# A two-layer graph network on 64 images: the first batch's convolution transform as TensorE products, its outputs finished by quarters

## The chip, the cores and the metric

The kernel runs on one core of a Trainium2 chip. The metric is device time in microseconds (us) of one execution, lower is better. Before the change it is 2314.8 us (median of three runs, 2313.39 to 2315.6). Runs are compared with runs of the kernel before on the same chip.

Engine names in the profile: PE is TensorE (matrix products and transposes), PEld its weight load, DVE VectorE, ACT ScalarE, POOL GpSimd, SP the engine that issues most loads.

## The reference, cut to what matters

There are 64 images of 256 nodes with 256 features. Each goes through two convolutions along the nodes, a distance-weighted message passing, a gated update, and a second layer of one aggregation with a layer norm.

```python
xc = jnp.transpose(x, (0, 2, 1))
h = jax.nn.relu(_bn(_conv1d(xc, conv1_w, 0), ...))       # 1 tap
h = _bn(_conv1d(h, conv2_w, 8), ...)                      # 17 taps: "conv2"
x_conv = jnp.transpose(jax.nn.relu(h + xc), (0, 2, 1))
s = x @ w_se.T + b_se                                     # 3 coordinates per node
A = jnp.exp(-dist) * mask                                 # dist from s
x_nmp = A @ jax.nn.relu(x @ w_msg.T + b_msg)
# gates r, z, n from [x_conv, x_nmp] and x; then the second layer (cut)
```

## The kernel before

conv2 is not computed tap by tap. Tiles of 32 nodes are taken to a transform domain (slots V, U, S and S2 of a large tile XF), multiplied there slot by slot with transformed filters on PE (`ps_k`), and taken back (the "inverse"). The transform, the merges of the products and the inverse are additions on DVE. Eight images form a batch and share this work: DVE's instructions cover all eight.

One product group uses three PSUM banks. The results leave them by `take`, one copy on ACT and two instructions on DVE:

```python
    def products(b, first, sums):
        p1, p2, p3 = bank("ps_k1"), bank("ps_k2"), bank("ps_k3")
        ...
        def take():
            nc.scalar.copy(k1, p1)
            nc.vector.tensor_sub(sl(re, 2)..., k1, p3)
            nc.vector.tensor_add(sl(im, 2)..., k1, p2)
```

All PSUM tiles of the kernel come from one pool of eight banks.

The convolution of the *next* batch is a generator that yields estimated costs. It is dealt out at ten points ("pumps") per image between the work of the images of *this* batch:

```python
    def cost(n):
        return 0.15 + 0.265 * n
    ...
        share, spent = (39.0 if b == 0 else 61.0) / len(todo), 0.0   # between two product groups of a batch
    ...
    for b in range(NB):
        coming = conv(b + 1) if b + 1 < NB else iter(())
        done, at, goal = 0.0, 0, BG * POINTS - 6
        def pump():
            nonlocal done, at
            at += 1
            while done < total * at / goal:
                t = next(coming, 1e9)
                if t is None:
                    break
                done += t
        for k in range(b * BG, (b + 1) * BG):
            ...                     # the image's own work, with ten pump() between
        for _ in coming:            # whatever is left is emitted here, in one block
            pass
```

`total` is not a constant. It is what batch 0's own convolution cost while it was emitted at the start:

```python
    first, total = conv(0), 0.0
    ...
        total += next(first)
        for i in range(n_groups):
            next(fl)                # one step of making the filters
            while total < FRONT * (i + 1) / n_groups and 0 not in STAGE:
                total += next(first) or 0.0
```

The "front" below means everything until the first gates: filters, batch 0's convolution, the first messages. A "seam" is the passage from the last image of one batch to the first of the next. There are seven.

## Time and profile before

| stretch of the kernel before | length, us | PE busy | DVE busy |
|---|---|---|---|
| start to first products (110.35) | 110.35 | 84.2 | 64.8 |
| products of batch 0 and merges (to 165) | 54.65 | 46.4 | 49.7 |
| inverse of batch 0 (to the first gates, 190.2) | 25.2 | 15.3 | 20.9 |
| one steady batch length (456 to 723) | 267 | 263.2 | 206.0 |

The last row is how the table is to be read: over 267 us PE did 263 us of work, so only work taken off PE or gaps of PE can shorten it. In the first three rows PE idles 44 us together; this is what the change is after.

### The profile page before, as it was taken

How to read it: one execution, taken by the hardware profiler on the slowest of the kernel's cores; microseconds unless marked ns; L12 is line 12 of the kernel's file. 1: busy time of each engine (PE TensorE's matmuls, PEld its weight loads, DVE VectorE, ACT ScalarE, POOL GpSimd, SP SyncE). 2: the span in 40 equal slices, each digit the busy share in tenths (PEclk: the TensorE clock that was granted, in tenths of full speed). 3: DMA queues.
4: the chain of work that ended last, by engine and by line, in shares of the span. 5: the costliest groups of instructions: out<-in, count | busy, mean ns of one | idle time of the engine just before them, and what ended most of it. 6: DMA issues, size and time to landing. Idle time of an engine off the chain costs nothing.

```text
span 2314.6 us, 24215 instructions
## 1 busy us (share of the span) xinstructions
PE 2225.2 (96%) x8262; PEld 1456.2 (63%) x8262; DVE 1685.2 (73%) x3212; ACT 766.0 (33%) x1577; POOL 468.7 (20%) x925
## 2 busy tenths in 40 slices
PE   7879999999999999999999999999999999999996
PEld 4565566666666666666666566665666656666663
DVE  2893998759794788829887498956889398874543
ACT  4514222442224321353224332253223532243332
POOL 1000221312122222202212131221222122121211
PEclk8998999999999999999999999999999999999998
DMA  5543152224323144221532234222433214321100
GB/s 176 156 161 114 59 170 67 85 94 130 118 73 109 50 137 132 74 100 37 169 99 73 101 106 143 75 96 69 136 105 101 94 43 151 113 78 37 46 23 14
DMA packets 211128, 226.66 MB, mean 98 GB/s; under 512 B 22087, under 2 KB 201790, under 8 KB 211006
## 3 DMA queue, kind: packets, MB, share of 16 engines
q1 hardware_dynamic: 188448, 191.14, 26.2%
q10 hardware_dynamic: 22558, 33.99, 4.2%
q8 instruction: 66, 1.08, 0.2%
q14 instruction: 56, 0.46, 0.1%
HBM read 179.22 MB, written 45.88 MB: 97 GB/s over the span
## 4 chain that ended last, share of the span: by engine, by line
PE 69%; DVE 21%; DMA 4%; issue 3%; POOL 2%; ACT 1%; ACTq 0%; SPq 0%; DVEq 0%; POOLq 0%
PE ps_rz L637 14%; PE ps_k L383 12%; DVE XF L103 8%; PE ps_n L649 7%; PE ps_rz L635 7%; PE ps_out L712 6%; PE ps_c L454 5%; PE ps_nmp L619 4%; PE ps_n L647 4%; PE ps_out L724 3%; PE ps_msg L575 3%; DVE w L103 2%; DVE XF L464 2%; DVE bst L654 2%; DMA w<-w2m 2%
## 5 line engine op out<-in xcount | busy, mean ns | idle before, releaser
L103 DVE SCALAR_TENSOR_TENSOR XF<-XF 128x512 f32<-128x512 f32 (+2 forms) x800 | 506.7, 664 | 7.0
L676 POOL TENSOR_SCALAR q<-mv 128x2 f32<-128x2 f32 x64 | 32.1, 502 | 1459.1 <-DVE mv L655 1459.1
L383 PE MATMUL ps_k<-w,XF 128*128 128x256 f32 x1316 | 302.1, 385 | 15.2 <-ACT AT L609 11.6
L383 PEld LDWEIGHTS ps_k<-w,XF 128*128 128x128 f32 x1316 | 248.5, 192 | 64.1 <-ACT AT L609 17.3
L650 DVE TENSOR_TENSOR gn<-ps_n,brzn 128x512 f32<-128x512 f32 x128 | 88.1, 688 | 239.4 <-PE ps_n L649 239.4
L641 ACT ACTIVATE rz<-rz 128x512 f32<-128x512 f32 x128 | 80.7, 631 | 509.9 <-DVE rz L640 509.9
L635 PE MATMUL ps_rz<-whh,xT 128*128 128x512 f32 x512 | 240.8, 592 | 0.0
L637 PE MATMUL ps_rz<-wih,xc 128*128 128x512 f32 x512 | 240.6, 592 | 0.0
L637 PE MATMUL ps_rz<-wih,nmp 128*128 128x512 f32 x512 | 240.6, 592 | 0.0
L712 PE MATMUL ps_out<-wrr,hT 128*128 128x512 f32 x512 | 232.8, 598 | 5.5 <-ACT hT L701 5.5
L640 DVE TENSOR_TENSOR rz<-ps_rz,brzn 128x512 f32<-128x512 f32 x128 | 87.2, 681 | 192.2 <-PE ps_rz L637 192.2
L637 PEld LDWEIGHTS ps_rz<-wih,nmp 128*128 128x128 f32 x512 | 97.3, 190 | 122.5 <-issue 122.5
L637 PEld LDWEIGHTS ps_rz<-wih,xc 128*128 128x128 f32 x512 | 97.2, 190 | 122.5 <-issue 121.5
L712 PEld LDWEIGHTS ps_out<-wrr,hT 128*128 128x128 f32 x512 | 98.1, 192 | 105.2 <-issue 89.6
L580 ACT ACTIVATE msg<-msg 128x512 f32<-128x512 f32 x64 | 40.4, 631 | 353.1 <-DVE msg L579 353.1
L575 PE MATMUL ps_msg<-wms,xT 128*128 128x260 f32 x512 | 134.1, 402 | 12.5 <-DMA adj<-in_adjT_dram 8.1
L635 PEld LDWEIGHTS ps_rz<-whh,xT 128*128 128x128 f32 x512 | 92.2, 190 | 64.5 <-issue 61.2
L647 PE MATMUL ps_n<-whh,xT 128*128 128x256 f32 x512 | 131.6, 379 | 0.0
L649 PE MATMUL ps_n<-wih,xc 128*128 128x256 f32 x512 | 131.4, 379 | 0.0
L649 PE MATMUL ps_n<-wih,nmp 128*128 128x256 f32 x512 | 131.4, 379 | 0.0
L360 DVE TENSOR_TENSOR XF<-XF 128x512 f32<-128x512 f32 (+3 forms) x128 | 125.2, 1004 | 1.8
L454 PE MATMUL ps_c<-xTc,w 128*128 128x512 f32 x256 | 118.1, 604 | 7.6 <-ACT xTc L446 7.6
(105 smaller groups left out, 3486.6 us busy)
## 6 DMA issues: line engine op xcount, KB each, us to landing
w<-w2m SPq DMA_DIRECT2D x105, 768.0 KB, 5.9
xn<-in_x_dram SPq DMA_DIRECT2D x32, 512.0 KB, 4.3
xt<-xTc ACTq DMA_DIRECT2D x32, 512.0 KB, 3.3
xT<-xt SPq DMA_DIRECT2D x64, 256.0 KB, 3.0
adj<-in_adjT_dram SPq DMA_DIRECT2D x64, 256.0 KB, 2.8
x<-in_x_dram SPq DMA_DIRECT2D x64, 256.0 KB, 3.1
xb<-in_x_dram SPq DMA_DIRECT2D x32, 512.0 KB, 4.9
out_dram<-y ACTq DMA_DIRECT2D x64, 256.0 KB, 2.2
```

Source lines behind the costliest of these rows:

```text
L103: nc.vector.scalar_tensor_tensor(o, in0, s, in1, op0=op0, op1=op1)
L360: (nc.vector.tensor_add if add else nc.vector.tensor_sub)(sl(o, n), sl(a, n), sl(b, n))
L383: nc.tensor.matmul(ps, X[:, slot, c * P:(c + 1) * P], w(m, c), start=(c == 0), stop=(c == C - 1))
L454: nc.tensor.matmul(ps, w1[:, c, o * P:(o + 1) * P], xTc[:, c, :], start=(c == 0), stop=(c == C - 1))
L575: nc.tensor.matmul(ps[:, :D + 4], XT[k][:, c, m * P:(m + 1) * P], wms[:, c, :], start=(c == 0), stop=(c == C - 1))
L619: nc.tensor.matmul(ps[:, d * N:(d + 1) * N], MSG[k][:, m, d * P:(d + 1) * P], AT[k][:, m, :], start=(m == 0), stop=(m == C - 1))
L635: nc.tensor.matmul(prz, XT[k][:, c, q], whh[:, c, 0:2 * D], start=(c == 0), stop=False)
L637: nc.tensor.matmul(prz, t, wih[:, i, 0:2 * D], start=False, stop=(i == 3))
L647: nc.tensor.matmul(pn[:, D:], XT[k][:, c, q], whh[:, c, 2 * D:], start=(c == 0), stop=(c == C - 1))
L649: nc.tensor.matmul(pn[:, :D], t, wih[:, i, 2 * D:], start=(i == 0), stop=(i == 3))
L650: nc.vector.tensor_add(RZ[k][1][:, n, :], pn, brzn[:, 2 * D:])
L712: nc.tensor.matmul(ps, hT[:, c, n * P:(n + 1) * P], wrr[:, c, :], start=(c == 0), stop=(c == C - 1))
```

## The change

The intent is to take batch 0's transform off DVE. TensorE multiplies the conv1 outputs with a constant matrix (47 slots by 8 tiles, 376 columns) between the filter steps, so that DVE has no splits to do in the front; the outputs of batch 0 are finished by quarters of the nodes, with x added by TensorE as a product with the identity. The merges of all batches are rewritten so that one instruction covers both halves. The diff is long; its core, cuts marked:

```diff
-FRONT = 66.0
+FRONT = (1, 1, 0, 1, 1, 0, 1, 0, 1, 1, 0, 1, 0, 1, 1, 0, 1, 1, 1, 0)
 ...
+        def transform(g, i):
+            for c in range(C):
+                pss = [bank("ps_dft") for _ in range(C)]
+                for n in range(C):
+                    nc.tensor.matmul(pss[n][:, :FT], xn[:, 2 * i + n, q], dft[:, :FT], start=True, stop=False)
+                ...                                  # two matmuls of 47 columns for the tiles' edges
+                for n in range(C):
+                    nc.vector.tensor_copy(X[:, :SLOTS - 1, e:e + TB], at[n])
 ...
-    def merge(re, im, size, phis, scales, tmp, new):     # one instruction for each half
+    def merge(re, im, size, phi, scales, tmp):           # one instruction for both halves
+        both = X[:, re:re + 2 * (im - re)].rearrange("p (b s) e -> p b s e", b=2)
+        ...
+            nc.vector.tensor_sub(tt, a, b)
+            yield cost(size)
 ...
-        share, spent = (39.0 if b == 0 else 61.0) / len(todo), 0.0
+        share, spent = 57.0 / len(todo), 0.0
 ...
+        if b == 0:
+            for q in range(4):
+                ...                                  # second and third stage of the inverse for this quarter
+                        nc.tensor.matmul(at, xb[:, j, e], ident, start=True, stop=False)
+                        nc.tensor.matmul(at, X[:, V + q + 4 * j, e], ident, start=False, stop=True)
+                yield None
+            return
 ...
+        for i, steps in enumerate(FRONT):
+            next(fl)
+            for _ in range(steps):
+                next(first)
-        total += next(first)
-        for i in range(n_groups):
-            next(fl)
-            while total < FRONT * (i + 1) / n_groups and 0 not in STAGE:
-                total += next(first) or 0.0
```

## The prediction

> **What bounds the kernel now.** I read the page first (engine shares and slices), then busy time in stretches of one batch of eight images (267 us), then the start in order of time, then one seam between batches.
>
> ```profile
> PE 2225.2 (96%) x8262; PEld 1456.2 (63%) x8262; DVE 1685.2 (73%) x3212; ACT 766.0 (33%) x1577; POOL 468.7 (20%) x925
> ...
> PE   7879999999999999999999999999999999999996
> ...
> DVE  2893998759794788829887498956889398874543
> ```
>
> PE is full from the fourth slice (58 us each) to the last but one; only the first three slices, where the filters are made and batch 0 is convolved, have gaps. The stretches say it in us (columns: length, PE, PEld, DVE, ACT, POOL, granted clock, DMA share, GB/s):
>
> ```profile
> 151.40:190.20 38.80, 20.68 (x77) 14.98 (x78) 34.09 (x67) 10.30 (x23) 7.15 (x17) 0.69 0.53 175
> ...
> 456.00:723.00 267.00, 263.24 (x991) 173.22 (x990) 205.99 (x394) 88.29 (x181) 60.08 (x114) 1.00 0.32 101
> 723.00:990.00 267.00, 263.93 (x975) 171.81 (x974) 207.79 (x396) 86.24 (x177) 60.07 (x114) 0.99 0.32 102
> ```
>
> In a steady batch PE idles 3 to 4 us of 267, though DVE has 206 us of work: that holds only because DVE's work for the next batch's convolution (transform, merges, inverse) is dealt out in small pieces between PE's work on this one. Where it stood in one block, after the products of batch 0 (151.4 to 190.2 us), DVE was busy 34.1 of 38.8 us and PE only 20.7. How the pieces are dealt out at a seam is seen in PE's order of time:
>
> ```profile
> 434.04 1.88 PE L637 MATMUL ps_rz<-wih,nmp 128*128 128x512 f32 x4
> 435.75 1.04 PE L528 MATMUL ps_xc<-ident,XF 128*128 128x128 f32 x8
> 436.63 1.03 PE L647 MATMUL ps_n<-whh,xT 128*128 128x256 f32 x4
> ...
> 439.22 1.04 PE L528 MATMUL ps_xc<-ident,XF 128*128 128x128 f32 x8
> ...
> 445.68 1.04 PE L528 MATMUL ps_xc<-ident,XF 128*128 128x128 f32 x8
> ```
>
> The last outputs of the next batch (ps_xc) come in eights between gate matmuls, with no wait, and are finished some 13 us before the first gate that reads them (458.84).
>
> **What the skill says.** "VectorE: DVE Perf Modes", "The TRN2 errata": an fp32 tensor_tensor takes (N+151)/0.96 ns, 691 ns at 512. The trace agrees (688 for gn, 686 for the transform's scalar_tensor_tensor), so one instruction on two halves saves only the fixed 151 cycles, an estimate of 0.16 us each. Same page, "Why PSUM operands drop a tier": fp32 from PSUM runs at 1x, so I count the new 376-element evictions at about (376+120)/0.96 = 0.5 us (an estimate; the trace has no such copy). "TensorE: Matmul & The Clock Gate", "What's actually happening": after some 3.4 us idle the array runs at half rate until it has been busy for 3.4 us, so each long stop should cost 1.7 us more. The trace agrees: after 8.06 us idle, 16 message records took 5.37 us, while two steady lots of eight start 1.86 us after their start each, 3.7 us. "Perfetto Trace Analysis", "Optimization Strategy" advises interleaving regimes with different bounds; that is what the order above does, and what I find undone below.
>
> **The change, part by part.**
>
> Front (0 to 110 us). Removed from DVE: 4 butterflies of 2048 (2.29 us each), the splits and half-spectrum butterflies, 50 to 60 us in all, and their interleaving with the filter scaling that PE waits for (15.9 us idle at L200). Added to DVE: 32 evictions of 0.5 us and 16 conv1 instructions of 0.65, 26 us. Added to PE: 8 transforms, each 4 matmuls of 376 columns and 4 of 47. A 512-column matmul takes 0.86 us (four in 3.43), that is 1.67 ns a column, so a transform is 4x0.63+4x0.08 = 2.8 us and all eight are 22.6. PE's front is then: filters 49 (74 blocks, four in 2.65 us), conv1 and transposes 17.2, transforms 22.6, together 89. The first filter step now stands behind bn1's row, the scaling of w1 and conv1, so it starts near 19 us instead of 12. From there 49+22.6+12 = 83.6, plus some 4 us for the last filter piece (its load is still queued behind six stores of 1 MB: 83.6 to 96.1 us now) and 2 or 3 of slow clock: products start at about 110, against 110.35 now. DVE then has no splits beside the products, but merges of 43 us against PE's 41, and reaches the inverse at about 162 instead of 165. The x adds (4 of 1.2 us, with 1.97 and 0.88 us of DMA wait) leave DVE; 64 fp32 matmuls of 0.21 us (13.7) replace 32 transposes of 0.11 (3.5) on PE, mostly between quarters, but with only two x buffers quarters 2 and 3 wait a load of about 5 us. Sum for the front: -3 us, give or take 8. It is a gain of DVE time where PE now takes over as the bound.
>
> Steady batches. PE's work is unchanged: same products, transposes, gates. DVE's merges become fewer instructions (about 32 saved, some 5 us a batch), which PE does not feel.
>
> Seams: here I expect the loss. The kernel paces the next batch's convolution by `total`, the summed cost of batch 0's steps: at point `at` of 74 it goes on until done reaches total*at/74. Before, total is summed over all of conv(0). After, the 20 front steps call next(first) without adding, and batch 0 has no splits, so total is too small. I had a copy of each kernel write the numbers out while building:
>
> - before: total 107.7, a later batch needs about 107.2; nothing is left at a seam.
> - after: total 57.9, a later batch needs 103.7; at the 80th point done is 63.2, and 40.6 units in 75 steps are left, which the loop after the batch emits in one block. It is the same at all seven seams.
>
> The order of the built program confirms it: at each seam DVE has 64 instructions in a row with nothing of the images between them (20 scalar_tensor_tensor and 4 x adds last), and PE has the last three product groups, then 32 transposes ps_xc together, then the gates of the next image, which cannot pass them. Durations from the groups by form:
>
> ```profile
> L103 DVE SCALAR_TENSOR_TENSOR XF<-XF 128x512 f32<-128x512 f32 x448 | 294.5, 686 | 5.0
> L103 DVE SCALAR_TENSOR_TENSOR XF<-XF 128x1024 f32<-128x1024 f32 x96 | 116.4, 1215 | 0.9
> L103 DVE SCALAR_TENSOR_TENSOR XF<-XF 128x256 f32<-128x256 f32 x256 | 96.5, 419 | 1.2
> ...
> L539 DVE TENSOR_TENSOR XF<-XF,xb 128x1024 f32<-128x1024 f32 x32 | 38.9, 1214 | 2.9 <-DMA xb<-in_x_dram 2.9
> ```
>
> The block is 44 of 512 elements, 9 of 1024 (the x adds among them), 11 of 256. Overlap of neighbours makes a row of 512s cost 0.65 each rather than 0.686:
>
> ```profile
> 168.41 6.00 DVE L103 SCALAR_TENSOR_TENSOR XF<-XF 128x512 f32<-128x512 f32 x9
> ...
> 174.92 4.90 DVE L103 SCALAR_TENSOR_TENSOR XF<-XF 128x512 f32<-128x512 f32 x8
> ...
> 184.67 1.23 DVE L539 TENSOR_TENSOR XF<-XF,xb 128x1024 f32<-128x1024 f32 x1 [1.97 <-DMA xb<-in_x_dram]
> ```
>
> So 28.6 + 10.9 + 4.4 = 44 us. The third and fourth x adds wait for a load that can start only when the first and second have freed their buffers (5.2 us from issue to use in the chain of batch 0): 4.5 us. DVE enters the block late: from the end of ps_n it still has gn, nn, w, statistics, messages, h, mask and y (about 17 us with the merges between), while PE needs 7.7 us to the end of the aggregation: a lag of 9. PE therefore gets to the next gates 9+44+4.5+1 = 58.5 us after its aggregation, and has in that time three product groups (5.1+5.1+4.3) and the transposes (3.4), 17.9 us of its own work. It stands still for about 41 us, plus 1.7 of half clock: 43 a seam, 301 for seven. I give back 14 (2 a batch) for steady gaps that vanish as DVE is less loaded inside a batch.
>
> Sum: 2315 - 3 + 301 - 14 = 2599; I say 2595.
>
> **Rivals.** (a) The intended gain: the front shortens by 20 to 40 us and the seams cost nothing, 2275 to 2295. For it: DVE is at nine tenths there and PE waits on its scaling. Against: PE's own sum is 89 us, and the order at the seams. (b) The front gains but the seams cost only 15 to 20 us each, since DVE runs ahead into the block: 2420 to 2450. For it: DVE would have 60 us of slack in a batch. Against: its queue is in order, and the instruction before the block reads the aggregation of the last image. (c) The seams cost more, because loads of the last product weights (5.9 us each, three buffers) or stopped ACT and POOL chains add to the block: 2620 to 2650. DVE comes to those products 24 us into the block, so the loads should be hidden.
>
> **Range and chances.** The block is the same at seven seams, so the error is seven times that of one: 37 to 48 us each gives 2555 to 2635, with the front's 8 us inside. A result below 2361 would need under 7 us a seam, which nothing in the order allows: slower 0.96; 0.02 for each other.
>
> **What would show it.** PE busy near 2250 us but about 87% of the span. Seven gaps in PE of 20 us or more, 300 us or a little more apart, ended by DVE's x add, with a granted clock near 0.7 there; the chain at each running through DVE's scalar_tensor_tensor. A steady stretch between seams as now. First products near 110 us, first gates near 187. I would be wrong if ps_xc at the seams waits for nothing, if the gaps are under 20 us in sum, or if the first gates come before 170 us.

## More of the kernel before

The prediction shows the profile lines. One view it does not show is PE's list of waits in the kernel before. Its columns are: engine, what is written, what it waited for, us in total, times, longest.

```profile
PE ps_tT L200 <- DVE ws L191: 15.9, 10, 2.6
PE ps_k L383 <- ACT AT L609: 11.6, 14, 1.1
...
PE ps_msg L575 <- DVE XF L399: 4.5, 12, 0.5
...
PE ps_k L383 <- DMA w<-w2m: 2.5, 5, 0.7
```

The first line is the front's filter making. The next two shown are the price of using the banks again: in steady batches a product or a message waits, 26 times, for a reader to leave its bank, 1.1 us at the most.

A new tile gets, nearly always, the bank that was freed longest ago in the order of the program (1289 of 1304 reuses in a build of this kernel; only 641 take the bank of eight tiles before), and PE must wait until that bank's last reader is done. So a product group that moves can get other banks, and wait for other readers.

## The result, and the profile after

The changed kernel takes 2599.57 us (median of four runs, 2598.19 to 2602.02), against 2314.1 us for the kernel before in the same rounds (2311.32 to 2315.6). The ratio is 1.1236, 95% interval 1.1217 to 1.1256: slower by 12%. Ratios in this document are the mean time of one kernel's fast runs over that of the other's of the same rounds, so not quite the ratio of the medians quoted. All outputs are right. The prediction, 2595 us with a range of 2555 to 2635, held.

First the page: engine totals, then PE, DVE and the granted clock in 40 slices of 65 us.

```profile
PE 2294.3 (88%) x8526; PEld 1520.9 (59%) x8526; DVE 1652.4 (64%) x3034; ACT 755.6 (29%) x1561; POOL 422.0 (16%) x924
...
PE   8979999599985999679994999949999499985997
...
DVE  3383776657774677837678377684776657776443
...
PEclk9989999799997999889997999969999799997998
```

PE's busy time grew by only 69 us, the span by 284. Among PE's nines, after the front, there are seven stops: 5, 5, 67 (one stop that falls on two slices), 4, 4, 4 and 5; the granted clock has a dip at each. Between them PE is as full as before. The stretches of the first seam and of what follows it (columns as in the prediction: length, PE, PEld, DVE, ACT, POOL, clock, DMA share, GB/s):

```profile
445.15:504.03 58.88, 24.12 (x101) 20.40 (x100) 51.08 (x86) 10.27 (x22) 8.00 (x16) 0.65 0.28 94
504.03:750.00 245.97, 244.10 (x881) 156.72 (x881) 151.24 (x281) 77.18 (x159) 45.29 (x98) 0.99 0.27 88
```

In 58.9 us at the seam PE does 24 us of work, DVE 51. In the 246 us after it PE idles 1.9 us. The seam in PE's order of time (start, length, then the group; in brackets the idle time before it and what ended that):

```profile
445.15 1.03 PE L406 MATMUL ps_k<-w,XF 128*128 128x256 f32 x4
448.68 15.74 PE L406 MATMUL ps_k<-w,XF 128*128 128x256 f32 x64 [2.49 <-DVE st L683]
495.32 3.65 PE L636 MATMUL ps_xc<-ident,XF 128*128 128x128 f32 x16 [30.91 <-DVE XF L647]
499.79 1.97 PE L636 MATMUL ps_xc<-ident,XF 128*128 128x128 f32 x8 [0.81 <-DVE XF L647]
502.30 1.94 PE L636 MATMUL ps_xc<-ident,XF 128*128 128x128 f32 x8 [0.54 <-DVE XF L647]
504.03 1.94 PE L741 MATMUL ps_rz<-whh,xT 128*128 128x512 f32 x4
```

The last product groups run together, then PE stands 31 us until DVE has added x, transposes, and only then come the next image's gates. The end of DVE's block at the same seam:

```profile
481.42 12.62 DVE L129 SCALAR_TENSOR_TENSOR XF<-XF 128x512 f32<-128x512 f32 x20
493.96 2.35 DVE L647 TENSOR_TENSOR XF<-XF,xb 128x1024 f32<-128x1024 f32 x2
498.50 1.23 DVE L647 TENSOR_TENSOR XF<-XF,xb 128x1024 f32<-128x1024 f32 x1 [2.19 <-DMA xb<-in_x_dram]
500.93 1.23 DVE L647 TENSOR_TENSOR XF<-XF,xb 128x1024 f32<-128x1024 f32 x1 [1.20 <-DMA xb<-in_x_dram]
```

These are the 20 instructions and four x adds that the prediction found last in the block, with two waits for an x load. PE's list of waits puts the seven seams into one line:

```profile
PE ps_xc L636 <- DVE XF L647: 229.0, 20, 31.1
PE ps_k L406 <- DVE st L683: 17.4, 7, 2.5
PE ps_k L406 <- DVE XF L422: 13.1, 7, 1.9
```

The first two lines lie at the seams and make 246.4 us, 35 a seam. The third, once in each batch between seams, comes up again below.

The gates resume after a seam at 504.03, 814.99, 1126.05, 1437.82, 1750.27, 2064.36 and 2374.91 us, so a batch takes 311.8 us on average. The kernel before takes 271.85 us, by the first finished outputs of each batch. Six differences of 40.0 us, and 37.6 us for the first seam (306.2 us from the first gates to those of the second batch, against 268.6), are 277 us. The first gates come at 197.8 us instead of 190.2 us, 7.6 us later. Together that is the difference of the two spans, 2598.7 against 2314.6, within 1 us.

So the front, which the change was made for, is slower too. Its stretches after the change (to the first products, to the inverse, two parts of the inverse):

```profile
0.00:114.60 114.60, 103.43 (x462) 72.78 (x463) 39.16 (x87) 49.32 (x104) 2.54 (x11) 1.00 0.46 135
114.60:167.40 52.80, 44.96 (x198) 38.64 (x197) 44.72 (x71) 5.15 (x10) 3.63 (x2) 0.92 0.78 251
167.40:177.00 9.60, 4.22 (x13) 2.91 (x12) 9.39 (x20) 1.97 (x4) 6.01 (x11) 0.68 0.01 2
177.00:197.80 20.80, 20.80 (x153) 19.42 (x153) 9.85 (x17) 10.77 (x23) 0.00 (x0) 0.93 0.44 139
```

DVE is relieved as intended, 39 us in place of 65 before the products. PE is now the bound there, with 103 of 115 us. In the last line PE works for every one of the 20.8 us before the first gates, on the quarters: the change moved the end of the front from DVE to PE.

### The profile page after: what moved, and what is told of

Same layout as the page of the kernel before. It is cut to its first block, busy times and chain, and to the rows that moved or that the text cites. A ratio compares the mean times of both kernels' runs of the same rounds, so it can differ in the third digit from the quotient of the medians.

```text
span 2598.7 us, 24615 instructions
## 1 busy us (share of the span) xinstructions
PE 2294.3 (88%) x8526; PEld 1520.9 (59%) x8526; DVE 1652.4 (64%) x3034; ACT 755.6 (29%) x1561; POOL 422.0 (16%) x924
## 4 chain that ended last, share of the span: by engine, by line
PE 74%; DVE 19%; DMA 3%; issue 2%; ACT 1%; SPq 0%; POOL 0%; ACTq 0%; DVEq 0%; POOLq 0%
PE ps_rz L743 17%; PE ps_rz L741 8%; PE ps_n L755 8%; DVE XF L129 8%; PE ps_k L406 7%; PE ps_out L818 7%; PE ps_nmp L725 4%; PE ps_n L753 4%; PE ps_c L534 4%; PE ps_out L830 4%; PE ps_msg L681 4%; DVE XF L324 2%; DVE XF L326 2%; DMA xb<-in_x_dram 1%; PE ps_dist L713 1%
## 5 line engine op out<-in xcount | busy, mean ns | idle before, releaser
L129 DVE SCALAR_TENSOR_TENSOR XF<-XF 128x512 f32<-128x512 f32 (+2 forms) x750 | 470.9, 662 | 6.8
L406 PE MATMUL ps_k<-w,XF 128*128 128x256 f32 x1316 | 316.3, 400 | 31.9 <-DVE st L683 17.4
L406 PEld LDWEIGHTS ps_k<-w,XF 128*128 128x128 f32 x1316 | 261.1, 201 | 80.4 <-issue 20.1
L782 POOL TENSOR_SCALAR q<-mv 128x2 f32<-128x2 f32 x64 | 40.8, 637 | 1556.0 <-DVE mv L761 1556.0
L636 PE MATMUL ps_xc<-ident,XF 128*128 128x128 f32 x224 | 51.4, 415 | 229.0 <-DVE XF L647 229.0
L741 PE MATMUL ps_rz<-whh,xT 128*128 128x512 f32 x512 | 246.1, 604 | 0.0
L636 PEld LDWEIGHTS ps_xc<-ident,XF 128*128 128x128 f32 x224 | 43.9, 221 | 236.8 <-issue 224.2
L819 ACT COPY hr<-ps_out 128x256 f32<-128x256 f32 x128 | 47.6, 372 | 318.3 <-PE ps_out L818 318.3
```

Of the source, the lines that this page charges most:

```text
L129: nc.vector.scalar_tensor_tensor(o, in0, s, in1, op0=op0, op1=op1)
L406: nc.tensor.matmul(ps, X[:, slot, c * P:(c + 1) * P], w(m, c), start=(c == 0), stop=(c == C - 1))
L636: nc.tensor.transpose(ps[:, j * P:(j + 1) * P], X[:, V + 4 * q + j, o * P:(o + 1) * P], ident)
L741: nc.tensor.matmul(prz, XT[k][:, c, q], whh[:, c, 0:2 * D], start=(c == 0), stop=False)
```

## The experiments

Theory A is that of the prediction: `total` is too small, and the block left over at each seam is the loss; the merges' new form costs PE nothing. Rival B: part of the loss lies in the new code itself (the transform, the quarters or the merges), and would stay if the pace were right. All runs of one job shared their runs of the kernel before: 2314.12 us for the first four (seven runs), 2315.27 for the second four, 2317.24 for the next three, 2316.08 for the last.

### The change with a total that fits

```diff
     for f in early:
         f()
+    total = 103.7          # what a later batch needs
```

> The changed kernel with one line added: total is set to 103.7, what a later batch's convolution costs. Theory (the wrong pace leaves a block at seven seams, 40 us each): the seven seams cost nothing, so 2600 - 278 = 2322, the rest being the front's loss of 7 us; 2312 to 2330. PE has no wait on the x adds beyond 5 us in sum and DVE's block of 64 is gone from the seams. Rival (something else of the change slows later batches, such as the merges' new form): it stays above 2400.

Measured: 2380.09 us (2377.17 to 2381.8), ratio 1.0282 (1.0267 to 1.0298). The seams are gone: in the window where the first seam stood, 445 to 504 us, PE is busy 58.4 of 59 us. But 66 us remain against the kernel before, where I expected some 8 (2322). The forecast of 2312 to 2330 failed, and the rival's "above 2400" is not reached either. PE's waits show a new first line:

```profile
PE ps_k L406 <- DVE XF L422: 33.5, 7, 4.8
PE ps_k L406 <- DMA w<-w2m: 8.6, 5, 2.9
```

Seven times, once a batch, a product waits for DVE's `take` of an earlier product. So A is right on the block and wrong in saying that nothing else costs PE time. What is it that remains?

### The merges alone

The kernel before with only the new merges and the smaller share (57 for 61; 35 for 39 in batch 0); the old front sums a total of 104.06 by itself, and nothing is left at a seam.

```diff
+    def merge(re, im, size, phi, scales, tmp):    # as in the change
-        share, spent = (39.0 if b == 0 else 61.0) / len(todo), 0.0
+        share, spent = (35.0 if b == 0 else 57.0) / len(todo), 0.0
```

> The kernel before with the new merges (real and imaginary part in one instruction) and nothing else; its own total comes to 104.1. Theory: PE bounds a steady batch, so 5 us less of DVE work a batch moves nothing there; only the inverse of batch 0 shortens: 2314 - 3, 2306 to 2316. Rival (DVE sets PE's small steady gaps of 3.5 us a batch): up to 20 us faster, 2294 to 2300.

Measured: 2371.09 us (2366.99 to 2376.21), ratio 1.0251 (1.0226 to 1.0276). This smallest part of the change, which removes DVE instructions, costs 57 us together with the smaller share; neither forecast held. In the profiled runs the spans differ by 51.6 us: PE stands 38.8 us longer (128.2 against 89.4 us, 30.3 of it for DVE's `take`), and its work takes 12.8 us longer (2238.0 against 2225.2 us for the same 8262 records). Where the stops come from is seen in PE's order in batch 1, first for this kernel:

```profile
317.35 0.70 PE L604 MATMUL ps_dist<-lr 4*128 4x256 f32 x4
317.98 1.14 PE L572 MATMUL ps_msg<-wms,xT 128*128 128x260 f32 x4
319.91 1.14 PE L572 MATMUL ps_msg<-wms,xT 128*128 128x260 f32 x4 [0.79 <-ACT AT L606]
320.89 1.89 PE L380 MATMUL ps_k<-w,XF 128*128 128x256 f32 x8
327.11 5.38 PE L380 MATMUL ps_k<-w,XF 128*128 128x256 f32 x16 [4.33 <-DVE XF L396]
```

and the same place in the kernel before:

```profile
319.37 0.70 PE L607 MATMUL ps_dist<-lr 4*128 4x256 f32 x4
320.00 1.13 PE L383 MATMUL ps_k<-w,XF 128*128 128x256 f32 x4
322.25 4.58 PE L383 MATMUL ps_k<-w,XF 128*128 128x256 f32 x20 [1.12 <-ACT AT L609]
326.68 1.04 PE L575 MATMUL ps_msg<-wms,xT 128*128 128x260 f32 x4
```

Before, the product group (`ps_k`, 24 records) stands between the distances and the messages. With the new merges it stands behind the messages, one pump later. In a build of this kernel its second and third bank are then those of the product group before it. The third is read by DVE's `take` (L396), which comes only after the gates' arithmetic, and PE waits 4.33 us. In the kernel before, the same two banks come from the distances, which ACT reads at once, and PE waits 1.12 us. After such a stop the 16 records that follow take 5.38 us where 20 take 4.58 us: the granted clock from 327 to 333 us is 0.72 in this kernel and 1.00 in the kernel before.

The Trainium skill, "Perfetto Trace Analysis", "Optimization Strategy", says that the same gap repeating on the engine that should be full can mean that there is not enough room for the next tile. The trace agrees on the place (seven waits, 30.3 us in all), though the number of banks is the same in both kernels.

### The change without the quarters, and without the transform

To see what the two other parts cost, each was left out of the paced change.

```diff
-        if b == 0:          # finish by quarters
+        if b < 0:           # run 1: batch 0 finished as before; transform on TensorE kept
```

> The changed kernel with total = 103.7, and batch 0 finished as before: x added by DVE, 32 transposes. The front's transform by TensorE stays. If the quarters (64 fp32 matmuls in place of 32 transposes, 10 us more of PE, against 4.7 us of x adds and 3 us of their waits on DVE) are what lost time after the products, this is 2 to 6 us faster than the paced kernel; if they gain as intended it is 3 to 8 us slower. I expect faster, 2317.

Measured: 2376.85 us (2370.87 to 2382.81), ratio 1.027 (1.0245 to 1.0294).

The other run is the kernel with the merges alone, plus the quarters for batch 0 and `total = 103.7`; the transform stays on DVE.

> The kernel before with the new merges and with batch 0 finished by quarters, x added by TensorE; the forward transform of batch 0 stays on DVE; total = 103.7. If the TensorE transform costs the front 4 us (products started at 114.6 against 110.4 us), this is 4 us faster than the paced changed kernel, about 2317; if the transform gains, slower than it. Products should start near 110 us, first gates near 192.

Measured: 2372.5 us (2367.79 to 2374.36), ratio 1.0248 (1.023 to 1.0266).

Both totals missed what I expected by 55 to 60 us, because both contain the new merges and the smaller share. The front of the second run did as forecast: products start at 109.2 us, the first gates come at 190.4. On top of those the transform on TensorE costs 5.8 us (2376.85 less 2371.09) or, with the quarters, 7.6 (2380.09 less 2372.5). The quarters cost 1.4 or 3.2. These differences are hardly larger than the spread of single runs, and the share of batch 0 differs too (57 in the runs with the transform, 35 in the others), so they are not exact; but all four have the same sign. No gain of either part is to be seen, even when the pace is right.

### The block alone

The kernel before, old merges and all, with only its pace made wrong by hand:

```diff
     for f in early:
         f()
+    total = 60.8
```

> The kernel before, with its old merges and front, and only its pace made too small by hand (total 60.8 in place of 107.7), so that 41.2 units of the next batch's convolution are left as one block at each of the seven seams. If the block at the seams is the whole loss of the change: seven gaps in PE of some 40 us, about 2590 us (2570 to 2615). If the loss came from the new front, the quarters or the merges: within 30 us of before.

Measured: 2575.06 us (2573.51 to 2577.23), ratio 1.1127 (1.1108 to 1.1145). A wrong number and nothing else costs 260 us, 37 us a seam. Its first wait line has the shape of the changed kernel's:

```profile
PE ps_xc L528 <- DVE XF L539: 244.9, 22, 32.4
```

### The share alone

The 57 us of the merges could come from the form of the instructions or from the place of the product groups. The share moves product groups without touching any instruction:

```diff
-        share, spent = (39.0 if b == 0 else 61.0) / len(todo), 0.0
+        share, spent = (35.0 if b == 0 else 57.0) / len(todo), 0.0
```

> The kernel before with its old merges, only the share 61 made 57 (39 made 35), which moves some product groups in PE's order to behind the message passing and to the end of an image. If the place of the product groups in PE's order is what cost 57 us with the new merges alone: slower than before by some tens of us, 2330 to 2380. If the form of the new merge instructions is what costs: 2308 to 2318, as before.

Measured: 2329.6 us (2327.34 to 2331.7), ratio 1.0064 (1.0049 to 1.0079): 14 us, just under the 2330 to 2380 that I expected. It moves the groups to other places than the merges run did, and the waits are of another kind:

```profile
PE ps_k L383 <- DMA w<-w2m: 19.7, 10, 2.9
...
PE ps_k L383 <- ACT XF L398: 8.6, 7, 1.2
```

So a shift of place alone costs something, but this run does not say that it explains 57 us. The new merges with the old share and their own total of 104.06 were not run, so how much of the 57 us is the share's stays open.

### The merges, and the whole change, paced as before

By building variants and listing PE's order I found that the new merges with the old share of 61 and a total of 107.7 (the value that the kernel before computes) put every product group of a steady batch where it stood before. Only some of the last transposes `ps_xc` stand a point or two elsewhere.

```diff
-        share, spent = (35.0 if b == 0 else 57.0) / len(todo), 0.0     # merges alone
+        share, spent = (39.0 if b == 0 else 61.0) / len(todo), 0.0
...
+    total = 107.7
```

> The kernel before with the new merges alone, shares kept at 61 and 39 and total set to 107.7, so that the product groups stand in PE's order as before. If the place decides: 2306 to 2318, the wait of the products on the DVE take under 8 us instead of 30.3. If the form of the merges costs: about 2371, as with the merges and the smaller share.

Measured: 2319.01 us (2317.07 to 2320.52), ratio 1.0018 (1.0003 to 1.0033). The same merge instructions cost 4 us in place of 57; that is 1 us above the range named for the case that the place decides, and far from the 2371 of the other. The wait for the take has left the products altogether, and that for filters has shrunk from 12.9 us to 1.5:

```profile
PE ps_k L380 <- ACT AT L606: 12.5, 14, 1.1
...
PE ps_k L380 <- DMA w<-w2m: 1.5, 4, 0.7
```

The whole change in the same way (share 57 kept for batch 0):

> The whole change, with total set to 107.7 and the share of later batches to 61, as in the kernel before: every product group of a steady batch then stands at the same place among the images' matmuls as before. If the place decides: seams and bank waits gone, only the front's 7 us left, 2315 to 2328. If the new merges' form costs: as in the first pace run, 2370 to 2380.

Measured: 2323.22 us (2320.03 to 2324.72), ratio 1.0035 (1.002 to 1.005). Two numbers bring the changed kernel from 12.4% slower to 0.35%. What is left, 8 us, is about what the front loses: its first gates come at 198.9 us, 8.7 us later than in the kernel before. So the form of the merges costs little; where they let the next product group fall is what costs. Share and total also move DVE's pieces among the images' work, so the two runs do not separate PE's order from DVE's; the wait lines speak for the banks.

### The front: loads and masks first

Why does the front not gain? In it PE stood 7.8 us before the first messages, which wait for a load queued behind 1.5 MB of gate weights, and DVE 4.25 and 2.28 us before the first two masks. So in that kernel I put the images' loads ahead of those weights and the masks later:

```diff
-    wih = weight(wihT, 2 * D, 3 * D, "wih", nc.sync, work)
     for k in range(3):
         load(k)
+    wih = weight(wihT, 2 * D, 3 * D, "wih", nc.sync, work)
-    early = [messages(0), messages(1), factors(0), distances(0), mask(0), factors(1), distances(1), mask(1), passing(0), messages(2)]
+    early = [messages(0), messages(1), factors(0), distances(0), factors(1), distances(1), mask(0), messages(2), mask(1), passing(0)]
```

> The whole change paced as the kernel before (the run before last of the earlier job, 2323.2 us), and in the front the images' own loads ahead of the 1.5 MB load of wih in their queue, and the first two masks later in DVE's order. In its profile PE stood 7.8 us before the first messages (a load) and DVE 4.25 and 2.28 us before the masks, while PE was then the bound from 177 us to the first gates at 199. If that tail is what keeps the front from gaining: first gates at about 191, 2313 to 2319 us. If the front is bound by DVE's inverse or by PE's sum anyway: no change, 2321 to 2325.

Measured: 2324.06 us (2322.37 to 2326.19), ratio 1.0027 (1.0015 to 1.004). A miss; the other forecast, no change at 2321 to 2325 us, held. It is 0.0008 of the ratio better than without, and the first gates come at 197.8 us, not 191. Both waits did shrink (3.4 us before the messages; 0.7 us before a mask), but PE's stop mostly moved. PE now stands 7.7 us, in place of 4.2, for `st`, which comes from DVE and POOL after the merges, and 1.7 us within the messages, so 12.8 us in all in place of 11.9. After that PE, not DVE, ends this stretch. The control, the same reordering in the kernel before:

> A control: the kernel before with the same reordering of loads and masks in the front. There DVE's chain through the inverse, and two x loads of 5 us, ended last, not PE, so I expect less of it: 2309 to 2316 us. If it gains as much as the changed kernel does (6 us or more), the reordering is worth the same to both and speaks for neither.

Measured: 2315.16 us (2314.26 to 2316.32), ratio 0.999 (0.9977 to 1.0002), no difference that these runs can tell.

### The front: less for PE

Next, two things were taken from PE's path. The transform makes only the 32 independent slots (256 columns), and DVE adds the 15 sums; and the load of the last filter piece is issued before the six 1 MB stores that it stood behind.

```diff
-FT = (SLOTS - 1) * TB
+FT = S * TB                    # 32 slots; the 15 sums are left out of the matrix
...
+        def sums(g):           # after each pair of images
+            for o, re, im, n in ((S, V, V + 8, 8), (S2, U + 8, U + 12, 4), (S2 + 4, U + 4, U + 6, 2), (S2 + 6, U + 2, U + 3, 1)):
+                ...
+                nc.vector.tensor_add(*v)
...
-                for f in range(0, NM, 8): ...   # stores of the first half at once
+                held.append((c, f, g))          # stores kept for two steps, after fetch of the last piece
```

> The same with two more changes in the front: TensorE makes only the 32 independent slots of the transform (256 columns in place of 376) and DVE adds the 15 sums, and the load of the last filter piece goes ahead of the six stores. If PE's sum bounds the front as I take it: 32 matmuls less 120 columns at 1.67 ns are 6.4 us less of PE, products start at about 108 in place of 115, 2305 to 2313 us, under the kernel before. If DVE's sums (some 6.5 us more, in a stretch where it was busy 17 of 50 us) or the loads take the place: 2313 to 2325.

Measured: 2316.73 us (2316.51 to 2321.39), ratio 1.0004 (0.999 to 1.0017). The first products begin at 106.0 us in place of 114.6 and the first gates at 189.9 in place of 197.8. The two changes were made in one run, but its trace tells them apart: a transform takes 2.70 us from start to start in place of 3.52, so eight save 6.6 us; the stop of 2.1 us before the last filter piece is gone, and a new one of 0.9 us, for DVE's sums, stands before the products. So PE's sum was most of the bound up to the products, as I took it, and the gain passes through to the first gates. The total missed the 2305 to 2313 us named for this and lies in the rival's range: it is the time of the kernel before, not better.

### x added by DVE

In that kernel DVE was done with the inverse at 177.7 us and PE worked until 190. So x was added by DVE again, quarter by quarter, and the third messages were put ahead of the masks:

```diff
+                nc.vector.tensor_add(sl(V + q, 4, 4), sl(V + q, 4, 4), xb)
-                        nc.tensor.matmul(at, xb[:, j, e], ident, start=True, stop=False)
-                        nc.tensor.matmul(at, X[:, V + q + 4 * j, e], ident, start=False, stop=True)
+                        nc.tensor.transpose(at, X[:, V + q + 4 * j, e], ident)
...
-             distances(1), mask(0), messages(2), mask(1), passing(0)]
+             distances(1), messages(2), mask(0), passing(0), mask(1)]
```

> The lean front of the last job (2316.7 us), with x added to a finished quarter by DVE (4 instructions of 1.2 us) in place of 64 fp32 matmuls on TensorE (13.7 us, replaced by 32 transposes of 3.5), and the third messages ahead of the masks. There DVE ended the inverse at 177.7 us and stood 9.9 us, while PE was busy 13.0 of the 13 us from 177 to the first gates at 190. If PE's work for x is what ends the front: DVE ends near 183, first gates near 185.5, 2311 to 2314 us, under the kernel before by 3 to 6 us. If the x loads (two buffers) or the masks hold DVE instead: first gates at 189 or later, 2315 to 2320.

Measured: 2314.63 us (2313.72 to 2316.99), ratio 0.9999 (0.9985 to 1.0014). The first gates come at 189.4 us, not 185.5: a miss again. PE's work fell as expected, and with it its clock:

```profile
177.67 3.67 PE L693 MATMUL ps_msg<-wms,xT 128*128 128x260 f32 x8
183.88 1.07 PE L632 MATMUL ps_xc<-ident,XF 128*128 128x128 f32 x8 [2.54 <-DVE XF L626]
184.78 3.27 PE L737 MATMUL ps_nmp<-AT,msg 128*128 128x256 f32 x8
188.40 1.13 PE L632 MATMUL ps_xc<-ident,XF 128*128 128x128 f32 x8 [0.34 <-DVE XF L626]
189.36 1.88 PE L753 MATMUL ps_rz<-whh,xT 128*128 128x512 f32 x4
```

The messages took 3.67 us here where eight of them take 1.92 in the changed kernel, because PE had stood before them: from 164 to 177.7 us it was busy 7.2 of 13.7 us, and the granted clock was 0.50 there and 0.71 in the 7.1 us that follow. DVE stood 2.76 and 1.17 us for these messages, which I had put in its way, and its last x add ended at 188.2 us, not 183. Thus no version that I ran beats the kernel before. This one, the lean front and the reordered kernel before equal it: their intervals hold 1.

## Why the prediction was right or wrong

The total was right: 2599.6 us against 2595. It was right for the main reason; that it came within 5 us is luck, since two terms were off in opposite directions by about the same amount.

**The step that carried it held.** That `total` becomes too small, that 40 units are left at each of seven seams, and that the next gates cannot pass the block: the wrong total alone costs the old kernel 260 us, and the right total and share give the changed one 276 us back (2599.57 less 2323.22).

**The terms of the seam.** From the end of the aggregation to the next gates I had 9 + 44 + 4.5 + 1 = 58.5 us. Measured at the first seam: DVE enters its block at 455.5 us, a lag of 10.3; the block runs to the end of the second x add at 496.3, and the remaining two adds are 2.5, so 43.3 in all; the waits for x are 3.4; from there to the gates it is 1.9. The sum is 58.9 us. The stop was sized at 43 us with its half clock, less 2 given back per batch, so 41. The period grew by 40.0, at the first seam by 37.6, and the seams make 277 us where I had 301 - 14 = 287. Of those 10 us too many, 7.6 - (-3) = 10.6 came back in the front.

**"The merges' fewer instructions, which PE does not feel": this step failed**, though the time does not show it. They change what the generator yields and so, with the smaller share, the place of some of the later product groups. Paced to leave nothing at the seams but with the share of the change, they cost 57 us, some 8 a batch; at the old places they cost 4. In the changed kernel the product groups of a batch fall elsewhere again, three of the eight into the block, and the wait for the take is 13.1 us in place of 30.3. PE idles only 1.9 us in the 246 between the first two seams. The size was off too: I had 32 instructions and 5 us of DVE a batch; the traces have 160 fewer in all eight batches (3052 against 3212), 20 a batch, and DVE is busy 1676 to 1678 us in place of 1685, about 1 us a batch.

**The front: -3 us predicted, +7.6 measured; this term was mis-sized, beyond the 8 us allowed for it, and its sign was wrong.** Two parts of the sum were too small. First, a transform: I had 2.8 us, four matmuls at 0.63 and four at 0.08. The trace of the changed kernel:

```profile
55.62 1.43 PE L482 MATMUL ps_dft<-dft,xn 128*128 128x376 f32 x4
56.98 0.30 PE L484 MATMUL ps_dft<-dft,xn 32*128 32x47 f32 x1
...
57.33 1.53 PE L482 MATMUL ps_dft<-dft,xn 128*128 128x376 f32 x4
```

From 55.62 to 56.98 two large matmuls run (each leaves two records), so 0.68 us each; from 56.98 to 57.33 two small ones, 0.17 each. A transform is 4 x 0.68 + 4 x 0.17 = 3.4 us and eight are 27.2 instead of 22.6. That is 4.6 us more, and the products start 4.6 us later than predicted (114.6 against 110). That the two agree is partly chance: the first filter step was also 2.7 us later, at 21.7 us instead of 19, and PE stood 2.1 us for the last filter piece where I had 4. Products to inverse took 52.8 us where I had 52. Second, from the inverse to the gates I had 25 us and 30.4 were needed. I had written that the products with x lie "mostly between quarters"; they do not, since DVE hands over the second to the fourth quarter faster than PE can finish them, and PE was busy for the whole of the last 20.8 us. The step "PE takes over as the bound" was right and should have been carried through to this stretch as well. Taking 120 of 376 columns from the transform, with the load brought forward, moved the gates 8 us earlier. One profile places these points only to a few us: the runs whose front is that of the changed kernel start the products at 114.6, 118.5 and 115.1 us and the gates at 197.8, 201.7 and 198.9, and the two with the front of the kernel before have the gates at 190.2 and 188.4.

**What would show it.** PE's total was to be near 2250 us at 87%; it is 2294 at 88%. In the whole change paced as before, without the stops, the same number of records (8526) takes 2249 us, so the stops also made PE's records longer. The seven gaps, the clock of 0.65 at a seam (near 0.7 was said), the x add that ends them and the chain through DVE are as written. The first gates at 187 are not.

**The rivals.** (a), a faster front with free seams, 2275 to 2295, is not reached even with the pace repaired (2323). (b), 15 to 20 us a seam, falls with the 40.0. (c), more through loads of product weights, does not appear: products waited 1.2 us for filter loads in the whole run.

## What to carry to other kernels

When one constant that paces a software pipeline is computed from the work of another part of the program, look at every place that feeds it before changing that part; here a change to the first batch cost 12% of the whole time, nearly all of it in the passages to the other seven, and a printed `total` of 57.9 against a need of 103.7 told it in advance. When buffers rotate, fewer instructions or a smaller estimate can move a producer by one position and make it wait for a late reader; compare the order on the busiest engine before and after, even for a part that lies on an idle engine. And when work is moved from one engine to another, sum the receiving engine in every stretch up to the end of the path, not only in the one that was to be relieved.

## What the Trainium skill lacked or had wrong

- "TensorE: Matmul & The Clock Gate", "Back-to-back issue gap", has a row for matmuls of 1 to 64 columns (about 60 cycles, an issue floor of about 25 ns) and does not say how fp32 compares. Here two fp32 matmuls of 47 columns, each with its own weight load and each leaving two records, start together and take 0.35 us, 0.17 each; two of 32 columns in the lean front take 0.34. So the time did not fall with the columns, and scaling by columns, which gave 0.08 us, was half of it. The floor in that row is for an isolated matmul; whether the matmul or its weight load sets the 0.17 us, the runs do not tell.
- No page has it that, with the same number of PSUM banks, the order of the work can make a repeated gap: 30.3 us of waits in seven stops at one order, none of that kind before a product at another, 2371 against 2319 us.
- The pages on which the prediction rested were right here: 376 columns from PSUM took 0.50 us (two copies in 1.00), and after the 31 us stop 16 transpose records took 3.65 us where eight take 1.04 in the kernel before.
